# Cross-attention's norms and key sums: products with 32 output rows side by side in the TensorE array, in place of full-width ones

## The chip, the cores and the metric

The kernel runs on one core of one Trainium2 chip, in one launch. The metric is device time in microseconds (us); lower is better. All data are float32. Five engines work side by side, each through its own instructions in order: TensorE (PE in the profile, with its weight loads shown as PEld), VectorE (DVE), ScalarE (ACT), GpSimd (POOL) and SyncE (SP), which here only issues transfers. DMA engines move the data between SBUF and DRAM.

## The reference, cut to what matters

One pre-norm decoder layer on x of 16 batches x 128 tokens x 1024 channels: a single-head self-attention, a cross-attention, and a feed-forward part whose weights are stored in 4 bits. The change lies in the cross-attention:

```
qh = softmax(Wq q, over the 64 channels of a head) * 64**-0.5      # 8 heads x 64, n = 1024
kh = softmax(Wk k, over n)                                          # k = v = the context
context = einsum(kh, vh);  out = einsum(context, qh)
out = Wo out + bo                                                   # 128 x 1024 per batch
norm = max(sqrt(sum(out * out, over the 128 rows)), 1e-12)
x = x + out / norm * g * sqrt(128)
```

Two sums run over the partitions of a tile, or end there: the **norms**, a sum of squares over the 128 rows for each of the 1024 columns, and the **key sums**, for each of the 512 key channels the sum of exp(Wk k) over n, by which the softmax of the keys divides.

## The kernel before, in words

The self-attention comes first (until about 290 us), then the cross-attention (about 290 to 760 us), then the feed-forward part, whose matrix products are done by two levels of Strassen-like combinations. The 4-bit weights are unpacked to DRAM by a generator, `prepare`, whose steps are spread over all stages: each step unpacks half a matrix on DVE (operations on tiles `pa`) or combines the halves (tiles `pc`), and SP or POOL stores the results.

In the cross-attention, batches are taken in the order 8..15, 0..7. For each batch a loop runs over four pairs of 128-column chunks; an iteration has a key unit of the next batch and a query unit of this one. Most instructions of PE, DVE and SP go through a helper (line 63) that keeps them in program order on their engine, so most groups in the profile bear L63 and are told apart by their tiles. The order is written out by hand with a list: `later(n, fn)` calls fn after n ticks, and `tick()` stands after each key unit and each query unit, eight ticks a batch. An engine meets the work in the order in which the ticks hand it out.

What happens to one batch, with the lines of the kernel before:

- `key_unit` (L729): products into PSUM `kq` (2 buffers), exp by ACT into `ek` (3 buffers). Two ticks later `use` (L747) multiplies `ek` with the context into `kx` and adds `ek` on DVE into `st["sum"]`, tile `ksum`, 128 x 2 x 512. After the fourth pair its two halves are added (`t[:, 0] += t[:, 1]`) and `mix` is put down for four ticks later.
- `mix` (L773): four products on PE with the sum's 128x128 chunks as weights and one column of `ones` as the moving operand give the key sums as 128x4 in PSUM; DVE copies them into `sums`, takes the reciprocal, and scales with it the product `mp` of `kc` and `g_sb`, written to `m_sb`. That product is written as two halves of 64 output rows each: for every r the halves e = 0 and e = 1 go to PSUM partitions 0 to 63 and 64 to 127.
- `query_unit` (L802): products into `kq`, exp by ACT into `qe` (3 buffers). Two ticks later `weigh` sums over the heads on DVE and takes the reciprocal, and POOL multiplies `qe` with it; four ticks after the unit `turn` transposes `qe` in 32x32 blocks on DVE into `kt` and SP stores it to DRAM (`kd`); one tick later SP loads it back as `qs` (5 buffers).
- `project_out` (L866): four `piece`s at the ticks `when[0..3]` multiply `m_sb` with `qs` into PSUM `mm` (3 banks for all uses); after every second piece ACT writes `y` (with the bias) and its squares `sq`. Both tiles have one buffer (pool `b_1`). At tick `when[4]` comes `norms` (L889):

```
for h in range(2):
    ps = bps.tile([P, 512], F32, name="mm")
    tensor.matmul(ps, ones, sq[:, ts(h, 512)], start=True, stop=True)
    nc.scalar.activation(sq[:, ts(h, 512)], ps, AF.Ln)
nc.scalar.activation(sq, sq, AF.Exp, scale=-0.5)
```

`ones` is 128x128, so each product writes the column sums to all 128 partitions at once. ACT turns them into 1/norm in place. One tick later each come `scale` (y times 1/norm, DVE), `add` (y into the residual X, DVE), `stats` (mean and variance of X, DVE and POOL), `row_shift`, and `turned`, which writes the normalised rows `xn3` on ACT, stores X by POOL, and puts down `turn_rows` for two ticks later (a transposition on DVE and four stores `xt` by SP).

The last batches run out beside the first blocks of the feed-forward part: there `beside` (L1579) ticks once after each of its products, 14 to a block. When the list is empty, `raise_flag` is put down, which tests all sums on DVE and counts on PE with `ones`; when the list is empty again, `attention_done` frees the pools and starts the third part of `prepare` (`rest`). From then on `beside` takes a fixed number of its steps after each product. The flag decides at the end whether the whole layer is computed again in a safer form; for the inputs here it is not.

The rest of the feed-forward part needs the prepared weights: SP loads them as `w`, PE multiplies into the banks `p`, DVE and ACT read the banks into `sg` and `h`. PE's next products need the banks free.

Of the kernel before, what the change touches and what calls it, by code (L numbers as in the profile page):

```python
# [11 lines left out]
F32 = mybir.dt.float32  # L12
I32 = mybir.dt.int32
AF = mybir.ActivationFunctionType
# [4 lines left out]
P = 128  # L19
# [47 lines left out]
def decoder_layer(  # L67
# [558 lines left out]
    def later(n, fn):  # L626
        pend.append([n, fn])
# [10 lines left out]
    if True:  # L638
# [11 lines left out]
        g_sb = bs.tile([P, HEADS, S], F32, name="g_sb")  # L650
        xbo_sb = bs.tile([P, 1], F32, name="xbo_sb")
        gs_sb = bs.tile([P, 1], F32, name="gs_sb")
        ones = bs.tile([P, P], F32, name="ones")

        batches = [p + i for p in PASSES for i in range(HB)]
        nc.sync.dma_start(wk_sb, xwk)
# [17 lines left out]
        def sums_tile(n, at, name):  # L674
            return sums[:, ds(at, n)] if plain else bsm.tile([P, n], F32, name=name)

        def raise_flag():

            within = [bsm.tile([P, 1], F32, name=f"within{n}") for n in range(2)]

            def test(n):
                op, limit, holds = (
                    (ALU.max, LIMIT, ALU.is_le),
                    (ALU.min, 1 / LIMIT, ALU.is_ge),
                )[n]
                vector.tensor_reduce(within[n], sums, AX.X, op)
                vector.tensor_scalar(within[n], within[n], limit, None, holds)

            def count():
                ps = bps.tile([P, 1], F32, name="mm")  # L690
# [38 lines left out]
        def key_unit(ctx, p, st):  # L729
# [17 lines left out]
            def use():  # L747
# [14 lines left out]
                elif p > 1:  # L762
                    vector.tensor_tensor(st["sum"], st["sum"], ek, ALU.add)
                if p == 3:
                    t = st["sum"]
                    vector.tensor_tensor(t[:, 0], t[:, 0], t[:, 1], ALU.add)
                    st["kc"] = b1.tile([P, HIDDEN], F32, name="kc")
                    nc.scalar.copy(st["kc"], st["ps"])
                    later(4, lambda: mix(st))

            later(2, use)

        def mix(st):  # L773

            D = DIM_HEAD
            ks = bps.tile([P, 4], F32, name="mm")
            for r in range(4):
                tensor.matmul(
                    ks[:, r : r + 1], st["sum"][:, 0, ts(r, P)], ones[:, 0:1], start=True, stop=True
                )  # L780
            ksum = sums_tile(4, B * 8 * HEADS + 4 * st["b"], "ksum")
            krec = bsm.tile([P, 4], F32, name="krec")
            vector.tensor_copy(ksum, ks)
            vector.reciprocal(krec, ksum)
            kc = st["kc"]
            mp = bps.tile([P, 4, S], F32, name="mm")
# [79 lines left out]
        def project_out(b, qs, st, when):  # L866
            out, bank = {}, {}

            def piece(h, part):
                if h == part == 0:  # L870
                    out["y"] = b1.tile([P, C], F32, name="y")
                    out["sq"] = b1.tile([P, C], F32, name="sq")
                if part == 0:
                    bank[h] = bps.tile([P, 512], F32, name="mm")
                ps, y, sq = bank[h], out["y"], out["sq"]
                for r in range(4):
                    tensor.matmul(
                        ps[:, ts(part, 2 * P)],
                        st["m"][:, r, :],
                        qs[2 * h + part].rearrange("p a (i r) j -> p r i a j", r=4)[:, r],  # L880
                        start=(r == 0),
                        stop=(r == 3),
                    )
                if part == 0:
                    return
                nc.scalar.activation(y[:, ts(h, 512)], ps, AF.Identity, bias=xbo_sb)
                nc.scalar.activation(sq[:, ts(h, 512)], ps, AF.Square, bias=xbo_sb)

            def norms():  # L889
                y, sq = out["y"], out["sq"]  # L890

                for h in range(2):
                    ps = bps.tile([P, 512], F32, name="mm")
                    tensor.matmul(ps, ones, sq[:, ts(h, 512)], start=True, stop=True)
                    nc.scalar.activation(sq[:, ts(h, 512)], ps, AF.Ln)
                nc.scalar.activation(sq, sq, AF.Exp, scale=-0.5)
                steps = (scale, add, stats, lambda: row_shift(b, vector), lambda: turned(b))
                for n, step in enumerate(steps):
                    later(when[5] + n * when[6], step)

            def scale():
                y, sq = out["y"], out["sq"]
# [51 lines left out]
        for k, b in enumerate(batches):  # L954
# [1 line left out]
            qs = {}  # L956


            if len(ahead) == 2:
                when = (14, 15, 16, 17, 18, 1, 1) if k < 13 else (13, 14, 15, 16, 17, 1, 1)  # L960
            elif ahead:
                when = (12, 13, 14, 15, 16, 1, 0)
            else:
                when = (10, 10, 11, 11, 12, 1, 1)
            project_out(b, qs, keys[b], when)
            if ahead:
                later(5, lambda n=ahead[0]: xns.update({n: rows(n)}))
# [2 lines left out]
            for n in (5,) if k < 12 else ():  # L970
                later(n, lambda: next(middle, None))

            for n, q in {B - 3: [(5, 5)], B - 2: [(3, 7), (7, 6)], B - 1: [(6, 4)]}.get(k, ()):
                later(n, lambda q=q: operand(q))
            for oc in range(4):
                if ahead:
# [63 lines left out]
    with ExitStack() as gs:  # L1040
# [872 lines left out]
```

## Time and profile before

| | |
|---|---|
| runs: median (lowest to highest) of 3 | 2226.76 us (2226.05 to 2232.44) |
| the profiled execution: span from its first to its last instruction | 2228.8 us |
| mean granted TensorE clock | 0.996 of full |
| PE, PEld, DVE, ACT, POOL busy, of the span | 98%, 69%, 70%, 23%, 25% |
| one batch of the cross-attention, from one `norms` on PE to the next | 31.23 us (twelve times, 31.22 to 31.24) |
| from 303.8 to 757.9 us: PE, DVE, ACT, POOL busy | 452.5, 370.8, 262.1, 169.1 of 454.1 us |

The profile gives no other time of the profiled execution; its span lies within the runs and is 2.0 us (0.09%) above their median.

How to read it. The end of a matrix product in the profile is modelled, so PE is judged by the distances between starts. One float32 product of the kernel shows as two MATMUL records (two passes), each with a weight load: "x4" of 128x512 is two products. A group's line names the output tile, then its inputs, then partitions x elements; "idle before" is what the engine waited for just before. The window figures are for stretches of the span.

### The profile page before, as it was taken

To read this page: it belongs to the slowest core of one execution; us is meant where nothing else is said; L and a number is where in the kernel's file an instruction comes from. 1 tells how busy PE (TensorE), PEld (TensorE's weight loads), DVE (VectorE), ACT (ScalarE), POOL (GpSimd) and SP (SyncE) were. 2 spreads that over 40 slices of the span, in tenths; PEclk is the share of its full clock that TensorE was granted. 3 is DMA by queue.
4 is the path that set the end of the run, shared out by engine and by line. 5 is a ranking of instruction groups with operands and counts; after the bars stand their busy time and mean duration, and the time that the engine had idled before them with its cause. 6 is when DMAs were issued, how large, how long until landed. Compare 5 with 4: busy or idle time off the path is not lost.

```text
span 2228.8 us, 24449 instructions
## 1 busy us (share of the span) xinstructions
PE 2192.9 (98%) x8500; PEld 1547.7 (69%) x8500; DVE 1563.4 (70%) x2119; ACT 508.5 (23%) x684; POOL 564.2 (25%) x442
## 2 busy tenths in 40 slices
PE   8999999999999999999999899999999999999998
PEld 7556555555555544444888488888887788888887
DVE  7897577888887637667799778787786645544462
ACT  2111235665556531111121112122121000000000
POOL 5453133333333300001354134444442000000000
PEclk9999999999999999999999999999999999999999
DMA  6435447777796748899544835465555965334631
GB/s 253 158 130 185 142 144 242 226 228 231 234 290 190 241 137 263 254 292 303 183 135 137 231 113 164 158 199 164 167 195 180 346 200 179 101 124 138 219 118 40
DMA packets 268725, 425.27 MB, mean 191 GB/s; under 512 B 28784, under 2 KB 130544, under 8 KB 268464
## 3 DMA queue, kind: packets, MB, share of 16 engines
q1 hardware_dynamic: 239584, 368.54, 52.7%
q0 software_dynamic: 10704, 35.92, 4.4%
q10 hardware_dynamic: 18304, 19.14, 2.7%
q8 instruction: 70, 1.15, 0.2%
q14 instruction: 63, 0.52, 0.1%
HBM read 265.62 MB, written 157.35 MB: 190 GB/s over the span
## 4 chain that ended last, share of the span: by engine, by line
PE 88%; DVE 6%; DMA 3%; issue 2%; SPq 1%; ACT 0%; POOL 0%; DVEq 0%; ACTq 0%; POOLq 0%
PE q L63 24%; PE po L1792 21%; PE p L63 11%; PE kq L63 10%; PE mm L63 8%; PE kx L63 5%; PE mm L397 4%; PE p L1166 2%; DVE pa L63 2%; PE mm L412 2%; PE mm L295 1%; DVE ti L63 1%; DMA wd<-pc 1%; PE tr L344 1%; DVE C L63 1%
## 5 line engine op out<-in xcount | busy, mean ns | idle before, releaser
L63 PE MATMUL q<-ti,li 128*128 128x256 f32 x1176 | 271.6, 380 | 2.9 <-DVE ti L63 1.4
L63 PEld LDWEIGHTS q<-ti,li 128*128 128x128 f32 x1176 | 222.5, 190 | 37.0 <-POOL li L63 4.5
L63 POOL TENSOR_TENSOR li<-w 128x512 f32<-128x512 f32 x98 | 141.2, 1443 | 342.9 <-DMA wd<-pc 235.2
L63 PE MATMUL p<-b,w 128*128 128x512 f32 x432 | 194.1, 602 | 12.5 <-DVE h L63 12.0
L825 POOL TENSOR_TENSOR qe<-qe,qrec 128x1024 f32<-128x1024 f32 x64 | 148.1, 2314 | 180.1 <-DVE qrec L63 156.0
L63 ACT COPY k<-q 128x512 f32<-128x512 f32 x147 | 86.0, 585 | 468.8 <-PE q L63 467.6
L1792 PE MATMUL po<-wc,lc 128*128 128x256 f32 x840 | 183.4, 379 | 0.0
L1792 PEld LDWEIGHTS po<-wc,lc 128*128 128x128 f32 x840 | 159.6, 190 | 21.8
L63 PEld LDWEIGHTS p<-b,w 128*128 128x128 f32 x432 | 82.9, 193 | 118.0 <-issue 100.9
L63 PE MATMUL p<-T,w 128*128 128x512 f32 x304 | 134.7, 592 | 0.0
L1792 PE MATMUL po<-wq,lq 128*128 128x256 f32 x560 | 126.7, 379 | 0.3 <-issue 0.3
L63 PEld LDWEIGHTS mm<-qs,m_sb 128*128 128x128 f32 x512 | 97.3, 190 | 40.1 <-issue 29.4
L63 DVE STREAM_TRANSPOSE kt<-qe 128x1024 f32<-128x1024 f32 x64 | 79.4, 1240 | 64.5 <-POOL qe L825 58.1
L63 PE MATMUL kq<-wq_sb,xn 128*128 128x512 f32 x256 | 120.3, 593 | 1.6 <-ACT qe L813 1.6
L63 PE MATMUL kx<-ek,cxt 128*128 128x512 f32 x256 | 121.8, 598 | 0.0
L63 PE MATMUL mm<-qs,m_sb 128*128 128x256 f32 x512 | 120.8, 379 | 0.0
L63 PE MATMUL kq<-wk_sb,cx 128*128 128x512 f32 x256 | 120.1, 592 | 0.0
L1792 PEld LDWEIGHTS po<-wq,lq 128*128 128x128 f32 x560 | 106.0, 190 | 15.9 <-issue 1.1
L397 PE MATMUL mm<-xnT,wqkv_sb 128*128 128x512 f32 (+1 forms) x320 | 113.2, 510 | 0.0
L63 POOL TENSOR_TENSOR li<-w,li 128x512 f32<-128x512 f32 x49 | 66.3, 1352 | 183.7 <-PE q L63 172.6
L63 DVE TENSOR_TENSOR pa<-pa,sz 128x1024 f32<-128x1024 int32 x86 | 108.8, 1265 | 2.4
L63 PEld LDWEIGHTS p<-T,w 128*128 128x128 f32 x304 | 57.8, 190 | 72.7 <-issue 72.2
(193 smaller groups left out, 3759.9 us busy)
## 6 DMA issues: line engine op xcount, KB each, us to landing
w<-wu SPq DMA_DIRECT2D x140, 256.0 KB, 3.5
lq<-h SPq DMA_DIRECT2D x140, 256.0 KB, 4.4
w<-wg SPq DMA_DIRECT2D x138, 256.0 KB, 2.9
kd<-kt SPq DMA_DIRECT2D x64, 512.0 KB, 3.7
qs<-kd SPq DMA_DIRECT2D x256, 128.0 KB, 3.5
h<-hc SPq DMA_DIRECT2D x80, 256.0 KB, 2.9
wq<-wd SPq DMA_DIRECT2D x70, 256.0 KB, 5.2
h<-h SPq DMA_DIRECT2D x60, 256.0 KB, 2.1
```

What stands on the lines that cost most here:

```text
L63: return lambda *args, **kw: self._tc.keep_in_program_order(fn(*args, **kw))
L295: tensor.matmul(ps, oT[:, d, ts(b % BPT, S)], wo_d[d][:, ts(h, 512)], start=(d == 0), stop=(d == 1),)
L344: nc.tensor.transpose(tr[:, j, :], xn[:, ts(4 * h + j, P)], ident)
L397: nc.tensor.matmul(ps[:, tokens], wqkv_sb[:, f, c, :], xnT[:, c, tokens], start=(c == 0), stop=(c == CC - 1),)
L412: nc.tensor.matmul(ps, xnT[:, c, ts(i, S)], wqkv_sb[:, 4:6, c, :], start=(c == 0), stop=(c == CC - 1),)
L825: nc.gpsimd.tensor_tensor(qe, qe, rec.unsqueeze(2).to_broadcast(wide), ALU.mult)
L1166: tensor.matmul(ps, wt[:, j, :], T[q][:, :, j], start=(first == q and j == 0), stop=(q in (2, 3, 4) and j == JC - 1), skip_group_check=True,)
L1792: nc.tensor.matmul(bank[:, i, :], l[:, ts(i, S)], w,  start=(start and c == 0 and i % 2 == 0), stop=(stop and c == len(pairs) - 1), skip_g ...
```

## The change

- `norms`: four products with a weight of 32 columns (`ones` is now 128x32), each over 256 of the 1024 columns of `sq`, write to partitions 0-31, 32-63, 64-95 and 96-127 of one 128x256 bank. ACT takes logarithm and exponential of 128x256 in place of 128x1024. So 1/norm stands on 32 equal rows for each quarter of the columns. SP stores one row of each (4 x 256) to a DRAM tile `rn_flat`, and one tick later (`spread`) loads it into `sq`, spread over all 128 partitions (512 KB). `scale` and what follows come later: 3, 4, 5, 6, 7 ticks after `norms` for the first twelve batches and the last, where it was 1 to 5; 2 to 6 for the batch k = 12, (2, 3, 3, 4, 5) for k = 13, and all at 2 for k = 14.
- `mix`: eight products with the 32 columns of `ones` as weights, of 128 columns each, over the four chunks c and both halves i of the sum. Each chunk writes to its own 32 partitions of a 128x128 bank, and the second half is added to the first in PSUM, so DVE's addition of the halves is gone. DVE turns the 128x128 in 32x32 blocks, back into the sum's tile, where the key sums stand in the first column of each block; then copy and reciprocal as before. For the first batch `mix` comes after three ticks, not four.
- `y` and `sq` are taken when ACT first writes them; the pieces of the last batch move from ticks (10, 10, 11, 11) to (11, 11, 12, 12) and its `norms` from 12 to 13; one operand of the feed-forward part (`operand(4)`) from tick 6 to 7.
- `raise_flag` is put down after the sixth product of the first feed-forward block, no longer when the list is empty. With the moved steps the list is empty after 18 products where it was after 20, and `rest` starts two products earlier; by the pattern of its steps, all of them then stand one step earlier among the products.

```diff
-        ones = bs.tile([P, P], F32, name="ones")
+        ones = bs.tile([P, Q], F32, name="ones")
...
                 if p == 3:
-                    t = st["sum"]
-                    vector.tensor_tensor(t[:, 0], t[:, 0], t[:, 1], ALU.add)
                     st["kc"] = b1.tile([P, HIDDEN], F32, name="kc")
                     nc.scalar.copy(st["kc"], st["ps"])
-                    later(4, lambda: mix(st))
+                    later(3 if st["b"] == batches[0] else 4, lambda: mix(st))
...
         def mix(st):
-            ks = bps.tile([P, 4], F32, name="mm")
-            for r in range(4):
-                tensor.matmul(
-                    ks[:, r : r + 1], st["sum"][:, 0, ts(r, P)], ones[:, 0:1], start=True, stop=True
-                )
-            ksum = sums_tile(4, B * 8 * HEADS + 4 * st["b"], "ksum")
+            ks = bps.tile([P, 4, Q], F32, name="mm")
+            parts = st["sum"].rearrange("p i (r c q) -> p i c r q", r=4, c=4)
+            for i in range(2):
+                for c in range(4):
+                    tensor.matmul(
+                        ks[ts(c, Q)], ones, parts[:, i, c], start=(i == 0), stop=(i == 1)
+                    )
+            kt = st["sum"][:, 0, ds(0, P)]
+            vector.transpose(kt, ks.rearrange("p r q -> p (r q)"))
+            kt = kt.rearrange("p (r q) -> p r q", r=4)
             krec = bsm.tile([P, 4], F32, name="krec")
-            vector.tensor_copy(ksum, ks)
+            ksum = kt[:, :, 0]
+            if plain:
+                ksum = sums_tile(4, B * 8 * HEADS + 4 * st["b"], "ksum")
+                vector.tensor_copy(ksum, kt[:, :, 0])
...
             def norms():
-                for h in range(2):
-                    ps = bps.tile([P, 512], F32, name="mm")
-                    tensor.matmul(ps, ones, sq[:, ts(h, 512)], start=True, stop=True)
-                    nc.scalar.activation(sq[:, ts(h, 512)], ps, AF.Ln)
-                nc.scalar.activation(sq, sq, AF.Exp, scale=-0.5)
+                ps = bps.tile([P, 2 * P], F32, name="mm")
+                for c in range(4):
+                    tensor.matmul(
+                        ps[ts(c, Q)], ones, sq[:, ts(c, 2 * P)], start=True, stop=True
+                    )
+                rn = sq[:, ds(0, 2 * P)]
+                nc.scalar.activation(rn, ps, AF.Ln)
+                nc.scalar.activation(rn, rn, AF.Exp, scale=-0.5)
+                flat = dram.tile([4, 2 * P], F32, name="rn_flat", tag="rn_flat", bufs=2)
+                def spread():
+                    sync.dma_start(sq, flat.rearrange("c n -> (c n)").partition_broadcast(P))
+                sync.dma_start(flat, rn[0:P:Q])
+                later(1, spread)
                 steps = (scale, add, stats, lambda: row_shift(b, vector), lambda: turned(b))
-                for n, step in enumerate(steps):
-                    later(when[5] + n * when[6], step)
+                for n, step in zip(when[5], steps):
+                    later(n, step)
...
-            if len(ahead) == 2:
-                when = (14, 15, 16, 17, 18, 1, 1) if k < 13 else (13, 14, 15, 16, 17, 1, 1)
-            elif ahead:
-                when = (12, 13, 14, 15, 16, 1, 0)
+            if k < 12:
+                when = (14, 15, 16, 17, 18, (3, 4, 5, 6, 7))
+            elif k == 12:
+                when = (14, 15, 16, 17, 18, (2, 3, 4, 5, 6))
+            elif k == 13:
+                when = (13, 14, 15, 16, 17, (2, 3, 3, 4, 5))
+            elif k == 14:
+                when = (12, 13, 14, 15, 16, (2, 2, 2, 2, 2))
             else:
-                when = (10, 10, 11, 11, 12, 1, 1)
+                when = (11, 11, 12, 12, 13, (3, 4, 5, 6, 7))
...
-                if not pend and plain and not flagged:
+                if plain and not flagged and n == 5:
                     flagged.append(raise_flag())
```

More of the change, by code (lines that the diff above doesn't have):

```diff
@@ L689, in count @@
             def count():
-                ps = bps.tile([P, 1], F32, name="mm")
+                ps = bps.tile([P, 1], F32, name="mm")[:Q]
                 for n in range(2):
@@ L869, in piece @@
             def piece(h, part):
-                if h == part == 0:
-                    out["y"] = b1.tile([P, C], F32, name="y")
-                    out["sq"] = b1.tile([P, C], F32, name="sq")
                 if part == 0:
                     bank[h] = bps.tile([P, 512], F32, name="mm")
-                ps, y, sq = bank[h], out["y"], out["sq"]
+                ps = bank[h]
                 for r in range(4):
@@ L885, in piece @@
                     return
+                if h == 0:
+                    out["y"] = b1.tile([P, C], F32, name="y")
+                    out["sq"] = b1.tile([P, C], F32, name="sq")
+                y, sq = out["y"], out["sq"]
                 nc.scalar.activation(y[:, ts(h, 512)], ps, AF.Identity, bias=xbo_sb)
@@ L971, in decoder_layer @@
                 later(n, lambda: next(middle, None))
-            for n, q in {B - 3: [(5, 5)], B - 2: [(3, 7), (7, 6)], B - 1: [(6, 4)]}.get(k, ()):
+            for n, q in {B - 3: [(5, 5)], B - 2: [(3, 7), (7, 6)], B - 1: [(7, 4)]}.get(k, ()):
                 later(n, lambda q=q: operand(q))
```

## The prediction

> **What bounds the kernel now.** I read the page's busy times and chain first, then the stretch of the cross-attention, then PE's timeline of one batch.
>
> ```profile
> PE 2192.9 (98%) x8500; PEld 1547.7 (69%) x8500; DVE 1563.4 (70%) x2119; ACT 508.5 (23%) x684; POOL 564.2 (25%) x442
> ...
> PE 88%; DVE 6%; DMA 3%; issue 2%; SPq 1%; ACT 0%; POOL 0%; DVEq 0%; ACTq 0%; POOLq 0%
> ```
>
> The chain that ended last is PE's. The stretch of the change says the same (busy us by engine, then clock, DMA share, GB/s):
>
> ```profile
> 303.80:757.90 454.10, 452.46 (x1575) 257.88 (x1574) 370.75 (x456) 262.12 (x298) 169.08 (x114) 1.00 0.76 231
> ```
>
> One batch on PE, from its norms on:
>
> ```profile
> 553.87 1.88 PE L63 MATMUL mm<-sq,ones 128*128 128x512 f32 x4
> 555.58 1.88 PE L63 MATMUL kx<-ek,cxt 128*128 128x512 f32 x4
> 557.30 1.88 PE L63 MATMUL kq<-wk_sb,cx 128*128 128x512 f32 x4
> 559.01 1.88 PE L63 MATMUL kq<-wq_sb,xn 128*128 128x512 f32 x4
> 560.73 0.95 PE L63 MATMUL mm<-ones,ksum 128*128 128x1 f32 x8
> 561.61 1.09 PE L63 MATMUL mm<-g_sb,kc 128*64 128x128 f32 x16
> 562.63 1.98 PE L63 MATMUL kx<-ek,cxt 128*128 128x512 f32 x4
> 564.46 1.88 PE L63 MATMUL kq<-wk_sb,cx 128*128 128x512 f32 x4
> 566.17 1.88 PE L63 MATMUL kq<-wq_sb,xn 128*128 128x512 f32 x4
> 567.89 1.89 PE L63 MATMUL mm<-qs,m_sb 128*128 128x256 f32 x8
> 569.62 1.88 PE L63 MATMUL kx<-ek,cxt 128*128 128x512 f32 x4
> ```
>
> No row has idle time before it, and starts follow each other at one pace: 0.43 us for a pass of 512 columns (1.72 / 4), 0.216 for 256 (1.73 / 8), so 0.108 for 128. What PE is spared here shortens the kernel, as long as no wait takes its place.
>
> **PE, the norms.** Before: four passes, 1.71 us. After: eight passes of 256 columns, two for each quarter of the array. The nearest row is the product of `kc` and `g_sb`: 64 output rows, written by turns to the two halves of the array. The records that start in its first 0.14 us, on PE and among the weight loads:
>
> ```profile
> 561.61 0.33 PE L63 MATMUL mm<-g_sb,kc 128*64 128x128 f32 x2
> ```
>
> ```profile
> 561.61 0.14 PEld L63 LDWEIGHTS mm<-g_sb,kc 128*64 128x64 f32 x2
> ```
>
> Two passes start at once, with their loads: one of each half, as two of one product would need the same columns; up to 561.80 there are four. So two run at a time: 16 passes in 8 x 0.108 = 0.86, where one after another they would need 1.73. The group takes 1.02 to the next start, so the change of shape costs 0.16, plus 0.11 in the next group (562.63 to 564.46 is 1.83, its like before took 1.72). Entering adds at most the time by which a record outlasts its stream, 0.592 - 0.429 = 0.16. In and out is 0.43 (0.27 if entering is free). I take four at a time for quarters, as the halves run two: 2 x 0.216 + 0.43 = 0.86, a gain of 0.85 per batch. Ends: if passes of quarters pair no better than strict program order lets them (below), 0.21; if they do not overlap at all, a loss of 8 x 0.216 + 0.43 - 1.71 = 0.45.
>
> **PE, the key sums.** Before: eight passes of one column, 560.73 to 561.61, 0.88 us: 0.11 each, the pace of weight loads of 128 columns. After: 16 passes of 128 columns, four at a time: 4 x 0.108 = 0.43, entering 0.16, first weights 0.05, and a change from quarters to halves before `g_sb`, which no row shows: between 0 and 0.16, I take 0.10, since leaving the halves looks like that (0.16 less the first weights). Sum 0.74, a gain of 0.14 (0.08 to 0.24).
>
> Here a page of the Trainium skill speaks against the change. The row is the one above: two starts at 561.61. The second is the other half's first pass, which stands third in program order, so it passed the second one. "TensorE: Matmul & The Clock Gate", Part 3 (What overlaps and what doesn't), says that products keep strict program order in start and end, and that a weight load overlaps a running product only in other row groups; here all rows are in use. By the rule the sum would be that of the first rival below or worse, by the row it is the forecast's.
>
> **PE in all.** 15 batches of norms 15 x 0.85 = 12.8, 16 of key sums 16 x 0.14 = 2.2. The last batch's norms stand among products of the feed-forward part in two pairs, each with 0.43 for its own way in and out: 2 x (0.43 + 0.43) = 1.72 for 1.71, no gain. The flag's two small products change shape too, 0.4 more. Sum: -14.6 us.
>
> **ACT** loses 2 x 0.60 + 1.06 for two pieces of 128x256, bounded by 0.2 and 0.6 each. ACT has 192 us free of 454; the worth is that 1/norm is ready about 1.3 us earlier.
>
> **DVE.** The addition of the halves goes: 2.16 us a batch in the mean (row below). The turn of 128x128 from PSUM is not in the trace; between the 0.15 of a 128x4 copy and the 0.69 of `m_sb` (128x512 from PSUM); an eighth of a 1.24 us `kt` plus that floor makes 0.3. DVE has 370.75 / 454.1 x 31.23 = 25.5 us a batch, then 23.6 in about 30.2.
>
> ```profile
> L63 DVE TENSOR_TENSOR ksum<-ksum 128x512 f32<-128x512 f32 x15 | 32.4, 2162 | 0.5
> ...
> L63 DVE SCALAR_TENSOR_TENSOR y<-sq,y 128x1024 f32<-128x1024 f32 x14 | 28.1, 2007 | 11.2 <-ACT sq L896 11.2
> ```
>
> **The new waits.** In us from the norms' start on PE. 1/norm is ready at about 4.6. SP then holds the small store; queued behind it are the loads of `cx` and `cxt` (used a batch later), four `qs` loads (used five or more ticks, some 19 us, later) and a `kd` store. SP's order then has the store `kd`, four stores `xt`, and the spread load: 0.4 + 0.4 + 2.2 + 0.35 + 1.9 of issue times, the `qs` loads waiting for their `kd` until about 7.3. So the load starts at about 12.2. Its landing is bounded by the quickest and slowest rows of like size:
>
> ```profile
> kd<-kt SPq DMA_DIRECT2D x60, 512.0 KB, 3.7
> ...
> cx<-in_cx SPq DMA_DIRECT2D x13, 512.0 KB, 5.3
> cxt<-in_cxt SPq DMA_DIRECT2D x13, 512.0 KB, 6.8
> ```
>
> 16 to 19, likeliest 17. DVE comes to `scale` at about 14.2: `m_sb` at 7.9 waits for PE, then `ksum` 1.2, unpacking 3.3, `kt` 1.2 and small ones. So `scale` waits 2 to 5 us each batch where it waited 1.1 for ACT. Behind it: a sum for POOL's weighing, `add`, the next `ksum`. What is free: 30.2 - 23.6 = 6.6, less some 3.6 in which `kt` waits for POOL whatever comes, so 3.0 us. A landing up to 17.2 costs PE nothing. Next late is ACT's `y` (one buffer): `add` ended at 10.8 and `y` was written at 21.1; now `add` ends at 20 to 23. ACT then holds a `kq` bank up to 2 us longer; PE wants it again 8.6 us later. The 8 MB more raise the main queue's 65% in this stretch to about 71%.
>
> **The end.** At k = 13 `scale` stands nearer to the load and DVE may wait 4 to 5 us ahead of the operand T4, which came 10 us early: 0 to 3 us for PE, I take 0.5. Where `rest` starts a step earlier, two waits of PE come into play:
>
> ```profile
> PE p L63 <- DVE h L63: 12.0, 2, 8.4
> ```
>
> They stand at 1057.7 and 1280.7 us, where unpacking on DVE stands ahead of the `h` that frees PE's banks; the second time DVE itself waited 9.4 us for a store (`wd<-pa`). A step earlier, the first place has combining (2.7) in place of unpacking (4 to 6), and the second store goes out about 3.4 us earlier, but one more unpacking (3.2) comes before the `h`. Bounds: both waits gone, -12; or one unpacking more in the way at each, +6. I take -2.
>
> Sum: -14.6 + 0.5 - 2 = -16.1, on the profiled execution's 2228.8: 2212.7. Nothing beside the span is known of that execution; it is 2.0 us above the runs' median, so 2211 for the median. This case alone spans 2202 to 2219 (key sums, entry and DVE terms at their ends, the feed-forward part from -8 to +5).
>
> **Rivals.**
> 1. The change does not do what it says: two passes of a product stand together in program order, and PE keeps to it. Then the norms take 5 slots (1.08 + 0.43 = 1.51, gain 0.2), the key sums 9 (0.97 + 0.31 = 1.28, loss 0.4): 16 x 0.2 + 0.4 = 3.6 us more, 2228 with the -2. The 64-row group speaks against it. No overlap at all would add 16 x (0.45 + 1.16) = 26, 2251, and is all but excluded by that row.
> 2. Slower: `scale` on DVE takes over as the bound. From a landing at 17.2 on, each us costs about 13 us in all. At 20.0 (a `cxt` landing, and 1 us more of queue): 13 x 2.8 = 36; 2226.8 - 14.6 + 36 = 2248. For it: the load stands last behind 2.5 MB of other transfers. Against it: `kd` behind the same traffic lands in 3.7.
> 3. The feed-forward part's preparation falls worse: +9 in place of -2, 2222.
>
> **How the numbers follow.** Forecast 0.70, rival 1 0.08, rival 2 0.13, rival 3 0.09. A difference of 0.3% (6.7 us) is what a measurement of this kernel can tell: faster is the forecast's 0.70, within 0.3% are rivals 1 and 3, 0.17, slower is rival 2, 0.13. The range 2200 to 2228 takes in the forecast's own, rivals 1 and 3, and leaves rival 2 out.
>
> **What would show it.** Right: four starts of `sq,ones` close together, twice, and about 0.86 us to the next group; key sums about 0.7; a batch of 30.2 us without PE waits; `y<-sq` waiting 2 to 5 us for a DMA. Wrong: starts spread over 5 slots or more (rival 1); PE waiting for ACT or DVE between 300 and 740 us, a batch above 31 (rival 2); waits of PE for `h` above 12 us in sum (rival 3).

## The result, and the profile after

The changed kernel takes 2255.2 us (median of 4 runs, 2251.7 to 2258.3) where the kernel before, on the same chip, takes 2229.0 (4 runs): a ratio of 1.0117, with a 95% interval of 1.0098 to 1.0136. It is slower by 1.2%. The profiled execution of it spans 2251.3 us, 22.5 more than that of before, and took 2253.4 in all.

The page of the changed kernel, PE's busy time and the chain by engine:

```profile
PE 2187.8 (97%) x8692; PEld 1528.7 (68%) x8692; DVE 1564.4 (69%) x2119; ACT 483.9 (21%) x668; POOL 564.5 (25%) x442
...
PE 75%; DVE 12%; DMA 6%; issue 2%; ACT 2%; POOL 1%; SPq 1%; DVEq 0%; POOLq 0%; ACTq 0%
```

PE is busy for 5 us less, yet carries 75% of the chain where it carried 88%. The stretch that the prediction used, 303.8 to 757.9 us, in the same columns:

```profile
303.80:757.90 454.10, 435.12 (x1686) 233.68 (x1685) 357.00 (x434) 234.72 (x277) 159.96 (x109) 0.99 0.76 237
```

Before, PE had 1.6 us free in these 454; now it has 19. One batch on PE, around its norms:

```profile
557.62 0.63 PE L63 MATMUL mm<-sq,ones 128*32 128x256 f32 x4
559.58 0.62 PE L63 MATMUL mm<-sq,ones 128*32 128x256 f32 x4 [1.33 <-ACT sq L893]
...
565.49 0.65 PE L63 MATMUL mm<-ksum,ones 128*32 128x128 f32 x16
566.06 1.09 PE L63 MATMUL mm<-g_sb,kc 128*64 128x128 f32 x16
```

The products do what the change wants: sixteen key-sum passes take 0.57 us to the next start, where eight of one column took 0.88. But PE stops in the middle of the norms for ACT's second square. The longest of PE's waits from 290 to 790 us:

```profile
PE mm L63 <- ACT sq L893: 17.1, 12, 3.3
PE p L1186 <- DMA w<-wg: 7.0, 1, 7.0
```

Before, neither was there. Who is really waited for is told by the chain of work between 540 and 592 us, which goes once round a batch (start, duration, what; pieces are left out at the dots):

```profile
539.85 6.09 DMA sq<-rn_flat
...
545.96 1.23 DVE y L63
...
548.60 1.11 DVE X L63
549.71 2.84 DVE ksum L63
...
556.65 0.12 DVE shift L63
...
556.79 1.59 ACT xn L152 x2
...
558.96 0.58 ACT sq L893
...
559.58 0.62 PE mm L63 x4
...
566.16 5.86 DMA qs<-kd
...
572.08 5.28 DMA sq<-rn_flat
577.38 1.23 DVE y L63
```

This is a closed loop of 31.4 us. The spread load ends late; behind it DVE does `scale`, `add`, the statistics and `shift` of that batch; ACT's normalised rows (`xn`, from `turned`) wait for `shift`; behind them, in ACT's queue, stand `y` and `sq` of the next batch; PE's norms wait for those. The load in turn stands behind SP's other transfers. From norms to norms a batch takes 31.5 to 36.8 us (the third to the twelfth), where the first two took 30.07.

SP's queue in the same batch (start, time until the last of a group was issued):

```profile
563.89 0.51 SPq L63 DMA_DIRECT2D rn_flat<-sq  x1
...
565.74 1.80 SPq L63 DMA_DIRECT2D qs<-kd  x4
567.58 0.43 SPq L63 DMA_DIRECT2D kd<-kt  x1
568.11 3.71 SPq L63 DMA_DIRECT2D xt<-kt  x4
572.08 0.34 SPq L63 DMA_DIRECT2D sq<-rn_flat  x1
```

The load is issued 14.5 us after the norms' start (557.62) and `y` starts at 19.8, where the prediction had 12.2 and 17. Its own store had landed long before, at 565.5. The chain names what held it last: `qs<-kd`, the second of the four `qs` loads, which landed at 572.01. In the trace SP's transfers here signal eight semaphores in rotation, and a transfer is issued only when the last one with the same semaphore, mostly eight places before it, has landed. So the last three `xt` stores followed the landings of `cx` (568.56), `cxt` (570.46) and the first `qs` (571.50), and in eleven batches, from the second to the twelfth, the load was issued 0.06 us after the landing of a `qs`.

**Where the 22.5 us come from.** Starts on PE, in us against the kernel before. "No load" is e2 below, which leaves the spreading out; "load ahead" is e13.

| mark | after | no load | load ahead |
|---|---|---|---|
| first norms | +1.1 | +3.0 | +2.1 |
| last product of cross-attention proper (`kq`) | +14.2 | -13.5 | -8.3 |
| first feed-forward product | +21.1 | -7.8 | -1.3 |
| last product of the part that waits for prepared weights (`q`) | +22.7 | -17.7 | -2.9 |

### The profile page after: what moved, and what is told of

Same layout as the page of the kernel before. It is cut to its first block, busy times and chain, and to the rows that moved or that the text cites. A ratio compares the mean times of both kernels' runs of the same rounds, so it can differ in the third digit from the quotient of the medians.

```text
span 2251.3 us, 24883 instructions
## 1 busy us (share of the span) xinstructions
PE 2187.8 (97%) x8692; PEld 1528.7 (68%) x8692; DVE 1564.4 (69%) x2119; ACT 483.9 (21%) x668; POOL 564.5 (25%) x442
## 3 DMA queue, kind: packets, MB, share of 16 engines
q8 instruction: 71, 1.16, 0.2%
## 4 chain that ended last, share of the span: by engine, by line
PE 75%; DVE 12%; DMA 6%; issue 2%; ACT 2%; POOL 1%; SPq 1%; DVEq 0%; POOLq 0%; ACTq 0%
PE q L63 23%; PE po L1812 21%; PE p L63 13%; PE mm L397 4%; PE kq L63 3%; PE mm L63 3%; DMA sq<-rn_flat 2%; PE p L1186 2%; DMA qs<-kd 2%; PE kx L63 2%; DVE pa L63 2%; PE mm L412 2%; DVE sums L63 2%; DVE ksum L63 1%; DVE kt L63 1%
## 5 line engine op out<-in xcount | busy, mean ns | idle before, releaser
L63 PE MATMUL p<-b,w 128*128 128x512 f32 x432 | 192.3, 598 | 13.6 <-DVE h L63 13.6
```

The costliest lines, as they stand in the source:

```text
L63: return lambda *args, **kw: self._tc.keep_in_program_order(fn(*args, **kw))
```

## The experiments

Three theories stood at the start. **Wait**: DVE's `scale` waits for the load, and what stands behind it comes late. **Order**: ACT's instructions, which the kernel doesn't pin, stand in another order than before (`y`, `sq`, `xn`, `y`, `sq` in a row ahead of the norms), and that order itself costs the time. **Traffic**: the added 8 MB slow the other transfers. Diffs are against the changed kernel unless said otherwise. All medians are us; ratios are to the kernel before, with 95% intervals.

### e1 and e14: ACT's order pinned

```diff
+    act = InOrder(tc, nc.scalar)
-    nc.scalar.activation(...)     # ek, kc, qe, y, sq, Ln, Exp, xn
+    act.activation(...)
```

> The changed kernel with ScalarE's instructions of the cross-attention kept in the order in which the program gives them (y and sq of the first half then stand before the exp of the query unit, as in the kernel before, and not bunched with the second half right ahead of the norms). Three theories of the 22 us that were lost. Order: the order on ScalarE is what makes PE wait for sq in the middle of the norms; then these waits (17.1 us, and some 5 us of lower clock after them) go and the time is about 2230. Wait: y and sq still have to wait for the late add of the batch before, so ScalarE stands there, and the exps behind it come late to PE: 2245 to 2255. Traffic: no change, 2255.

2251.5, ratio 1.0103 (1.0086 to 1.0120). PE no longer stops inside the norms, but waits elsewhere. One wait was new: 8 us at 262 us, before the first norms. e14 makes the same edit in the kernel before.

> The kernel before with ACT's instructions in the order in which they are written, nothing else. In both kernels of the change with that order, PE waited 8 us at 262 us for ek and reached the first norms 10.6 to 11 us late. If that is the price of the fixed order, it is here too: first norms 10 to 11 us late and 2234 to 2240; then the kernel e1 gained about 14 us in the batches and not 4. If it is the change's (its early mix), this kernel is as before within 3 us.

2239.0, 1.0043 (1.0026 to 1.0060), the first norms 10.1 us late. PE, at the start of its cross-attention:

```profile
261.41 2.93 PE L63 MATMUL kx<-ek,cxt 128*128 128x512 f32 x3 [7.62 <-ACT ek L63]
```

So pinning costs 10 us by itself, and from the first norms to the last `kq` e1 takes 413.5 us where the changed kernel takes 425.7 (before: 412.6). ACT's order carries about 12 us of the loss there; but 413.5 is still 17 above what the products allow (e2). Order is the way by which lateness reaches PE, not its source: in e2, where nobody waits for a load, ACT's order is that of before without a pin, and in e3 and e4 it is so ahead of the norms (a `qe` changes places elsewhere).

### e2, e3 and e4: without the load, and with a load that nobody reads

```diff
-                flat = dram.tile([4, 2 * P], F32, name="rn_flat", tag="rn_flat", bufs=2)
-                def spread(): ...
-                sync.dma_start(flat, rn[0:P:Q])
-                later(1, spread)
```

e2 also puts the steps back to 1 to 5 ticks after the norms; e3 keeps the late steps; e4 keeps store and load, but loads into a tile of its own (`wide`) that nothing reads, and leaves the query sums out of the flag's test to make room. None of the three scales by the right norms.

> The changed kernel without the store and the spread load of the norms (left out: scale reads what stands in sq, so the output is not the reference's), and with the steps after the norms 1 to 5 ticks later as in the kernel before. All three theories: about 2212 to 2218, that is the products' gain of 14.6 us alone, give or take 5 for the preparation of the weights that starts at another product. If it stays above 2225, the products themselves gain nothing.

> As the run without the spread (left out in the same way), but with the later steps of the changed kernel. Wait and order: the load is what makes scale late and what made the order on ScalarE another one, so nearly as fast as with the early steps, 2212 to 2220. If the later steps alone do it (y and sq have one buffer): 2240 to 2250. Traffic: 2212 to 2220.

> The changed kernel with the store and the spread load kept, at the same places on SP, but the load goes into a tile that nobody reads, and scale reads what stands in sq (left out: the spreading of the norms; the flag's test leaves out the query sums, to make room). Traffic: as slow as the changed kernel, about 2255, since all transfers are there. Wait and order: no wait for the load is left on VectorE, 2212 to 2222.

| | median | ratio | first norms to last `kq` |
|---|---|---|---|
| before | 2229.2 | 1 | 412.6 |
| e2, no load, early steps | 2212.9 | 0.9931 (0.9914 to 0.9947) | 396.1 |
| e3, no load, late steps | 2220.4 | 0.9961 (0.9947 to 0.9975) | 398.4 |
| e4, load unread, late steps | 2222.8 | 0.9973 (0.9962 to 0.9983) | 400.4 |
| the change | 2255.2 | 1.0117 (1.0098 to 1.0136) | 425.7 |

The transfers cost 2 us, the late steps 2 us there and some 5 later; waiting for the load costs 25 us there and 32 in all. Wait stands; Traffic, as the added bytes alone, falls. e2's batches take 30.07 us against 31.23: the narrow products are worth 1.16 us a batch. One batch's norms in e2, eight passes, 0.57 us to the next start (1.72 before):

```profile
548.78 0.64 PE L63 MATMUL mm<-sq,ones 128*32 128x256 f32 x8
```

### e5, e6 and e13: the same load, earlier

e5 issues it right behind its store, so SP stands still until the store has landed; e6 does both in ACT's queue; e13 only puts it first among the next step's transfers, ahead of the `kd` store and the four `xt`:

```diff
-                later(1, spread)
+                spread()                           # e5; e6 with nc.scalar.dma_start
+                pend.insert(0, [1, spread])        # e13
```

> Against the changed kernel only the place of the spread load is moved: SP issues it right behind the store of the norms (and so stands still until the store has landed), not a step later behind the kd store and the four xt stores. Nothing is left out, and the bytes are the same. Wait theory (DVE's scale waits for a load that is issued 14.5 us after the norms' start): the load is issued at about 7.5 us and lands at 11 to 13, before DVE comes to scale at about 14, so the wait y<-sq for a DMA falls from 27.9 us to below 5, PE's stalls in the middle of the norms go, and the time is that of the kernel whose load nobody waited for, 2222 to 2228. Traffic theory (the added transfers themselves cost the time): the bytes are there, so 2250 to 2258. A third, that SP is needed elsewhere: with SP held about 2 us a batch, kd stores and qs loads come late and PE waits for qs: 2230 to 2245 with waits of PE for a DMA.

> As the kernel with the load right behind the store, but both go through ACT's queue, so that SP has nothing of it and ACT stands still until the store has landed. Wait theory: again below 5 us of waits for the load, and 2222 to 2228 if ACT's standing still (about 2 to 2.5 us a batch, in which qe and ek wait and their banks with them) is covered by the 8 us after which PE wants such a bank again; up to 2240 if not. Traffic theory: 2250 to 2258.

> The changed kernel with one thing moved: the spread load stands first among the transfers of the next step, ahead of the kd store and the four xt stores, not behind them. SP no longer has to wait for the store itself. Wait theory: the load is issued about 10 us after the norms' start in place of 14.5 and lands at 13 to 15, as DVE comes to scale; y<-sq waits for it below 8 us in sum (27.9), PE's waits in the middle of the norms go, and the time is near that of the kernel whose load nobody waited for: 2221 to 2226. Rival: landing, not issue, is what is late (the stretch's DMA traffic): the wait falls by less than half, and the time stays above 2240.

e5: 2227.7, 1.0005 (0.9995 to 1.0015); PE now waits for `qs`, 5.4 us in three, as the third theory had it in part. e6: 2233.2, 1.0024 (1.0014 to 1.0033); ACT stands still for the store, and PE waits for `ek` ten times, 10.1 us in all. e13: 2228.7, 1.0005 (0.9995 to 1.0014), with its first norms to last `kq` in 402.2 us, within 2 of e4. Issuing one transfer some 6 us sooner takes 26 us off the kernel. One batch on SP, and one of PE's waits from 290 to 760 us, in e13:

```profile
554.67 0.50 SPq L63 DMA_DIRECT2D rn_flat<-sq  x1
...
558.46 0.38 SPq L63 DMA_DIRECT2D sq<-rn_flat  x1
```

```profile
PE mm L63 <- ACT sq L893: 0.7, 1, 0.7
```

The load is issued 8.5 us after the norms' start (549.95), no longer behind a landing, and the wait for the squares has gone from 17.1 us to 0.7. In its new place it takes 8.0 us to land (5.3 in the batch above), so `y` starts at 16.5 in place of 19.8: on these 3 us a batch the 26 hang. Batches take 30.4, not e2's 30.07: ACT's second square still comes a little late, and the second pair of quarters starts 0.33 to 0.41 us behind the first (second to eleventh batch), where in e2 all four start together. The median is above what was expected (2221 to 2226); two waits outside the batches stay (e9 to e15), and that at the first feed-forward weights is 7.1 us here, 3.7 in e4.

### e7: two buffers for `sq`, with ACT pinned

```diff
-                    out["sq"] = b1.tile([P, C], F32, name="sq")
+                    out["sq"] = b1.tile([P, C], F32, name="sq", bufs=2)
-                vector.scalar_tensor_tensor(y, sq, 1e12, y, ALU.min, ALU.mult)
+                vector.scalar_tensor_tensor(sq, sq, 1e12, y, ALU.min, ALU.mult)
```

with e1's edit; the flag's test leaves the query sums out.

> The load stays as late as in the changed kernel, so scale still waits for it; but ACT's order is fixed as written, and y and sq no longer wait for add: scale writes into sq, sq has two buffers, and y is free once scale has read it. To make room the flag's test leaves the query sums out. If the way from the wait to PE is the single buffer of y and sq (the next batch's y and sq on ACT come late, PE's norms behind them), this takes most of it away: 2222 to 2232, and ACT's waits for y fall from 59 us to below 15. If it is DVE's own time (what stands behind scale on DVE comes late: the key sums' reading, kt, m_sb), buffers do not help: 2243 to 2253.

2247.3, 1.0085 (1.0068 to 1.0102); first norms to last `kq` 414.5, no better than e1's 413.5. ACT's waits of `y` for DVE fall from 59.1 us in e1 to 32.7, not below 15 as expected: the one `y` is free of `add` now, but still waits for `scale`. What went bought no time, so the wait for `add` is not the way to PE; what a second `y` would do is not shown. With ACT's rows out of the way, the loop closes from the load through DVE and POOL; shares of the chain between 540 and 592 us in e7:

```profile
by line: POOL qe L831 14.3%; DVE ksum L63 13.5%; DVE qden L63 12.9%; DMA sq<-rn_flat 11.5%; DVE kt L63 9.9%; issue 8.4%; SPq L63 5.2%; DVE bnst L63 4.6%; DVE sq L63 4.6%; DVE X L63 4.3%; DVE pa L63 3.8%; DVE sums L63 3.7%; DVE qrec L63 2.2%
```

### e8 and e11: the key sums, and what DVE does not get back

e8 is the kernel before with the new key sums alone; e11 is e5 with the copy of the sums for the flag made by ACT (`nc.scalar.copy`), so that DVE's reciprocal reads the turned tile.

> The kernel before with the key sums of the change alone: four products of 32 output rows, their turn in 32x32 blocks and the copy of 4 columns, and no addition of the halves on DVE. Norms, their step and all times of steps as before. By the prediction's price PE gains 16 x 0.14 = 2.2 us, and DVE's 2.16 us a batch of addition go: 2225 to 2228. Rival: the copy of 4 columns out of SBUF, 1.7 us in the changed kernel where the copy from PSUM took 0.15, stands between the key sums and m_sb, and takes back what the addition gave; PE's own gain is unchanged by it since DVE is not the bound, so again about 2227, with DVE's busy time nearly that of before. If this kernel is slower than before by over 3 us, then the key sums carry a part of the loss that I had put down to the spread load.

> The kernel with the load right behind the store (2227.7), but DVE takes the reciprocal of the turned key sums directly, and their copy for the flag (128x4, 1.4 to 1.7 us a batch on DVE where a copy out of PSUM took 0.15) is made by ACT. Contention theory: that copy starts with POOL's product of qe and ends with it (568.35 to 570.24 beside 568.31 to 570.21), so it waited for POOL; the reciprocal, which stands in its place and reads SBUF too, then takes 1.4 to 1.9 in place of 0.18, or the next ones do, and DVE's busy time in cross-attention falls by less than 5 us; time 2225 to 2229. Rival: the copy itself is slow (its source has a stride of 32 columns): the reciprocal stays at 0.2, DVE gets back some 20 us and PE's waits for m_sb go: 2218 to 2224.

e8: 2230.9, 1.0010 (1.0001 to 1.0020), above the 2225 to 2228 expected, though its batches take 31.02 (0.21 less): the runs don't show those 3 us. e11: 2229.2, 1.0008 (0.9998 to 1.0018). What e11 tests is seen in DVE's groups of the changed kernel between 290 and 760 us (busy, then mean ns), and in one batch of it, DVE beside POOL:

```profile
L63 DVE TENSOR_TENSOR ksum<-ksum,ek 128x1024 f32<-128x1024 f32 x30 | 56.8, 1892 | 0.0
L63 DVE COPY sums<-ksum 128x4 f32<-128x4 f32 x14 | 23.7, 1693 | 0.5
```

```profile
568.35 1.89 DVE L63 COPY sums<-ksum 128x4 f32<-128x4 f32 x1
```

```profile
568.31 1.90 POOL L830 TENSOR_TENSOR qe<-qe,qrec 128x1024 f32<-128x1024 f32 x1 [3.96 <-DVE ksum L63]
```

A copy of four columns lasts exactly as long as POOL's product beside it. In e8 it takes 0.17 in the 12 batches where POOL does not run then, and 1.09 to 1.87 in the other three. `ksum<-ksum,ek`, 1186 ns before, is 1892 here, and the `y<-sq` that was 2007 is 1222 (now it waits 27.9 us for the load instead). So some of DVE's operations with SBUF operands are held while POOL's product runs, and which of them bears it depends on the time. The 2162 ns of the removed addition were largely such waiting. In the kernel before, it takes 2.27 us beside POOL's product in 14 batches, ending 0.55 us behind it, and 0.69 in the one where POOL is idle:

```profile
548.12 2.27 DVE L63 TENSOR_TENSOR ksum<-ksum 128x512 f32<-128x512 f32 x1
...
738.72 0.69 DVE L63 TENSOR_TENSOR ksum<-ksum 128x512 f32<-128x512 f32 x1
```

```profile
547.15 2.69 POOL L825 TENSOR_TENSOR qe<-qe,qrec 128x1024 f32<-128x1024 f32 x1 [2.81 <-DVE qrec L63]
```

Per batch these took 2.16 + 2.01 + 2 x 1.19 + 0.15 = 6.7 us before and 1.22 + 2 x 1.89 + 1.69 + 0.26 (the turn) = 7.0 after: DVE got nothing back. In e11 the reciprocal takes 0.18 in all 15 batches, in 13 of them beside POOL: not every operation is held, against one of the two things I had expected, and DVE now waited longer for PE (14.6 us ahead of the turn, e5 8.7). The Trainium skill ("SBUF — State Buffer", Who interferes with whom) has the rule: DVE and GpSimd share one pair of ports, which one instruction holds to its end; DVE's operations with two SBUF inputs and its copies in two-port modes need it, others do not. These rows agree with it (that the copy runs in such a mode, no row shows), and the prediction should have read its DVE rows by it.

### e9, e10, e12, e15 and e16: the rest of the gain

In the profiles, e5 has 4.7 us in hand at the last `kq` (e13 8.3) and ends 3.6 ahead; by the medians it ends level, and single runs of the kernel before differ by 6 us. Two waits take part of it. One, which the kernel before does not have, is in the changed kernel (7.0 us), in e13 (7.1) and in e2 (5.8); ACT and PE of the changed kernel:

```profile
768.04 1.02 ACT L818 ACTIVATE qe<-kq 128x1024 f32<-128x1024 f32 x1 [4.84 <-DVE kt L63]
768.06 0.82 ACTq L1111 DMA_DIRECT2D w<-wg  x2
```

```profile
773.07 6.22 PE L1186 MATMUL p<-b,w 128*128 128x512 f32 x8 [7.05 <-DMA w<-wg]
```

ACT's queue issues the first feed-forward weights only behind an exp that waits for DVE. The other is PE's wait for `h` near 1280 us. Edits on e5: e9 puts the last batch's steps at (2, 3, 3, 4, 5); e10 issues those weights from POOL's queue; e12 has both and e11's. On e13: e15 puts store and load of the last two batches into ACT's queue, with e9's steps; e16 adds e11's edit.

```diff
+                queue = nc.scalar if b in batches[-2:] else sync      # e15
+                queue.dma_start(flat, rn[0:P:Q])
-                when = (11, 11, 12, 12, 13, (3, 4, 5, 6, 7))
+                when = (11, 11, 12, 12, 13, (2, 3, 3, 4, 5))          # e9, e12, e15, e16
-            load_weights(nc.scalar if n == 0 else nc.sync)
+            load_weights(nc.gpsimd if n == 0 else nc.sync)            # e10, e12
```

> The kernel with the load right behind the store (2227.7), and the steps behind the last batch's norms earlier: scale, add and the rest 2, 3, 3, 4, 5 ticks after the norms in place of 3, 4, 5, 6, 7, so that the preparation of the feed-forward weights starts two products' blocks sooner. Feed-forward theory (of the loss that stays when the load is early, most is one wait of PE for an h of DVE near 1278 us, 10.9 us, which is 2.7 us where the steps stand early): the wait falls to 3 to 6 and the time to 2219 to 2223. Rival: the wait moves with the phase of the preparation by chance and not with those two ticks: 2225 to 2232, another wait of 8 to 12 us.

> The kernel with the load right behind the store (2227.7), and the first feed-forward weights issued by POOL's queue in place of ACT's. There ACT issues them only behind an exp that waits 4.84 us for DVE's kt, and PE stands still for 4.6 us at 751.6. If ACT's queue is the cause, the wait at the first feed-forward product goes from 4.6 to below 1, and with the slower clock after it the time falls by 4 to 6: 2222 to 2224. Rival: the place in memory of these weights, or the stretch's DMA traffic, holds them: no change, 2226 to 2229.

> All three edits on the kernel with the load right behind the store. Nothing left out. If each is worth what its own theory says and they add up: about 2227.7 less 6 (feed-forward wait) less 5 (first weights) less 0 to 2 (copy) = 2215 to 2218, faster than the kernel before by 0.4 to 0.6%. If the waits only move: 2224 to 2230.

> The kernel with the load ahead of xt, and for the last two batches the store and the load in ACT's queue (in SP's they stand behind loads of weights that wait up to 19 us for a buffer), with the last batch's steps 2, 3, 3, 4, 5 ticks after the norms. Feed-forward theory: DVE's waits for the last two loads (6.6 and 5.7 us) go, the preparation starts some 8 us sooner, the wait near 1280 us falls from 11 to 3 to 6 us, and the time is 6 to 9 us below the kernel with the load ahead of xt: 2213 to 2219, faster than before. Rival: the wait near 1280 us stands where DVE's and SP's preparation has other limits (stores and loads of its own), and PE's gain is given back there whatever starts sooner: 2221 to 2228.

> The kernel e15 (load ahead of xt, last two batches' load in ACT's queue, last steps early) with the copy of the key sums for the flag on ACT, DVE taking the reciprocal of the turned sums directly. If what hid e11's gain was the wait near 1280 us, which is 2.5 us in e15: cross-attention is 2 to 4 us shorter and this time it stays: 2217 to 2220.5. If DVE waits for PE in the copy's place as it did in e11, or the wait for the first feed-forward weights grows by what cross-attention gains: 2221 to 2225.

| | median | ratio |
|---|---|---|
| e9 | 2231.5 | 1.0014 (1.0004 to 1.0023) |
| e10 | 2232.2 | 1.0022 (1.0012 to 1.0032) |
| e12 | 2231.3 | 1.0015 (1.0006 to 1.0025) |
| e15 | 2222.4 | 0.9973 (0.9961 to 0.9986) |
| e16 | 2223.8 | 0.9976 (0.9966 to 0.9986) |

e9, e10 and e12 missed. In e10 the weights came later still: POOL's queue issues them at 751.1, behind a product that waits for DVE as the exp did, and PE waits 9.3. In e9 the wait near 1280 fell from 10.7 to 2.3 (expected: 3 to 6), but a new one of 5.6 came at 820, where DVE had waited 9.5 for the last batch's load and `h` stood behind it. e15 takes that load past the weights' loads, in which SP stands up to 19 us: the preparation starts at 818.7 (before 841.6, e13 833.8). The waits near 1280 are, in the kernel before, in e13 and in e15:

```profile
1280.70 5.44 PE L63 MATMUL p<-b,w 128*128 128x512 f32 x8 [8.45 <-DVE h L63]
```

```profile
1277.35 5.91 PE L63 MATMUL p<-b,w 128*128 128x512 f32 x8 [10.97 <-DVE h L63]
```

```profile
1272.86 5.39 PE L63 MATMUL p<-b,w 128*128 128x512 f32 x8 [2.35 <-DVE h L63]
```

So PE comes to this wait 5.9 us sooner in e13 than before (1266.4, before 1272.3), but `h` frees it only 3.4 sooner: part of PE's gain was given back to a preparation that had moved less. e15 keeps it: 0.27% faster than the kernel before, and the fastest here that leaves nothing out. By its time it lies in the range that was put down for the rival (2221 to 2228), though the wait shrank as the theory had it. e16 shows no gain from moving the held copy. Kept open is the first wait: e15 still has 7.2 us of it, and no run took it away.

## Why the prediction was wrong, point by point

- **PE's products: right.** Predicted 0.85 a batch for the norms and 0.14 for the key sums; e8's batches give 0.21 for the key sums (31.23 to 31.02) and e2's 1.16 for both, so 0.95 for the norms with the key sums in place. e2's median is 2212.9 where the sum without the late load would be 2211; that it comes so near is in part luck, as its feed-forward part gained 9.9 us (taken: 2) and the first weights' wait of 5.8 was in no sum. Where both squares are ready, the eight passes of one batch's norms start within 0.26 us (in e2 in all batches but the last, in the changed kernel in the first two), so four quarters run at once, and rival 1 is out. The strict order that the Trainium skill gives ("TensorE: Matmul & The Clock Gate", Part 3, What overlaps and what doesn't) does not hold here. In e2 all four quarters start within 0.02 us and their second passes from 0.24 on; in e13, with the same products in the program, the second passes of the first two quarters (0.24) start ahead of the other two quarters (0.33 and later). One of the two orders is not the program's, and the measurement decides.
- **The failed step: "A landing up to 17.2 costs PE nothing", with a landing "likeliest 17".** The load was issued 13.4 to 14.5 us after the norms in the steady batches and `y` began at 18.7 to 20.1, and later still in four; waiting for it cost 25 us in the batches (the change against e4). Two terms were short: the store went out at 5.8 to 6.3 (taken: 4.6), and the four `xt` took 3.7 us to issue (taken: 1.9), since they and the load followed the landings of earlier transfers, which the sum did not have. In the first batch, which has no `xt` ahead of it, the load was issued at 8.6, in the second at 13.5, in the third at 15.8: each batch hands its lateness on, since SP's, DVE's and ACT's are one loop. I had worked out one batch with its neighbours on time. Nor is a landing within 17.2 quite free: in e13 `y` begins at 15.8 to 16.8 in the second to tenth batch, and these take 30.4 us, not 30.07.
- **DVE's free 3.0 us: wrong.** The removed addition's 2.16 us was counted as work; most of it was DVE being held beside POOL, and it came back in the copy and in `ksum<-ksum,ek` (6.7 us became 7.0). A free time of 30.2 - 25.5 - 3.6 = 1.1 us was left.
- **"Next late is ACT's `y` (one buffer)": wrong way.** In the changed kernel ACT's `y` waits for no DVE instruction from 290 to 760 us; `xn` does, for `shift`, 20.9 us. The moved step `turned` falls into the tick of the next batch's second `y` and `sq`, one tick ahead of its norms, and ACT, whose order is not pinned, took `xn` ahead of them. Of a moved step I had counted the DMAs, not its ACT instructions, ahead of which and behind which they then stand.
- **Rival 2 was the case, and its price was near, in part by luck.** It said 2248 for a landing at 20.0. Landings of 19 to 20 gave 2255: 23.5 us in the batches (425.7 less e13's 402.2) where it had 36, and 7 at the first weights, which nobody had. Its way, through `scale` on DVE, was right; that ACT's order carries some 12 us of it, it did not have.
- **The end, 0.5: mis-sized.** The wait at T4 did not come; the 7 us for `w` did, because ACT's queue issues it behind the last exp.
- **The feed-forward part, -2: it was +1.5.** One wait (3.5) went, the other grew from 8.4 to 13.6. e2 shows -9.9 and e13 -1.5: which it is depends on when the preparation starts against PE, and rival 3 was right that it can eat what came before.

## What to carry to other kernels

An instruction's duration is not always its work: before a removal is credited, see what ran beside it on the engine that shares its ports, and ask who will bear that wait next. The round trip through DRAM cost 8.2 us in the issuing queue (store at 563.9, load at 572.1) and 5.3 for its own landing: into such a sum goes what stands ahead of the load, with the landings for which the queue itself stands still; put the load ahead of stores that nobody waits for. When a wait is added in a loop over batches, follow it once round until it meets itself: a lateness that the next batch inherits is not absorbed by a slack counted for one.

## What was not expected of the hardware

- How much of DVE's time is such holding, and how small an operation can bear it: a copy of 128x4 within SBUF takes 0.17 us, and 1.89 when POOL's product runs beside it.
- A wait of PE can bring the granted clock down to half for a while, and its length alone does not tell whether. In the changed kernel it did so after waits of 2.42 us (until 399.55) and 3.31 us (until 690.41) inside the norms, not after one of 2.56 us (until 656.41); the rows below show it (the clock is the third number from the end). e13 has no such stretch in its batches. With those at the two long waits, from 768 and 1294 us, the half clock stands for 34.1 us, in which PE is busy for 18.5; in the kernel before it is 10.2 and 7.0. By half of the busy time, an estimate, it costs 9 us here and 3.5 before, so some 6 of the 22.5 us are PE being slower behind its waits.

```profile
399.30:402.70 3.40, 3.15 (x7) 1.31 (x8) 2.60 (x3) 3.07 (x5) 0.59 (x2) 0.50 0.76 250
656.00:660.00 4.00, 3.58 (x11) 1.58 (x12) 2.60 (x3) 3.95 (x5) 1.19 (x2) 1.00 0.91 251
689.50:696.30 6.80, 5.89 (x10) 2.35 (x11) 3.66 (x4) 5.13 (x7) 2.89 (x2) 0.50 0.48 155
```
